# A planner's price for a change of the matmul tiling, extended to the second half of a four-layer kernel

## The chip, the cores and the metric

The kernel runs on one core of a Trainium2 chip. The metric is the device time of one execution in microseconds (us); where several executions are given, it is their median. Engines are named as in the profile: PE is TensorE (PEld its weight loads), DVE is VectorE, ACT is ScalarE, POOL is GpSimd, and SP issues most of the DMAs.

## The reference

A sequence of 2048 tokens of width 128 goes through four pre-norm layers. Each of them adds an attention-like block and then a feed-forward block to the stream `x`:

```python
x = L0_attn_x                                    # (1, 2048, 128), fp32
x = x + L0_attn(layernorm(x))                    # 16 heads of 8, softmax over all 2048 keys
x = x + L0_ffn(layernorm(x))                     # 128 -> 512 -> 128, gelu
x = x + L1_attn(layernorm(x))                    # 16 heads of 64, softmax over all 2048 keys
x = x + L1_ffn(layernorm(x))                     # gated, integer weights, 384 hidden
x = x + L2_attn(layernorm(x))                    # each token attends to itself and its two neighbours
x = x + L2_ffn(layernorm(x))                     # top-1 of 8 experts, 128 x 128
x = x + L3_attn(layernorm(x))                    # memory with a gradient step, a recurrence over
                                                 # chunks of 64 tokens: 32 chunks, in order
x = x + L3_ffn(layernorm(x))                     # top-2 of 8 experts and a shared one, 176 hidden
```

Everything after L1's attention is cheap for a token, but L3's memory makes the chunks wait for one another: chunk c starts from the state that chunk c-1 leaves.

## The kernel before

One Python function, `body`, writes the instructions of all engines. What it writes is fixed before anything runs, and each engine takes its instructions in the order in which they were written. That order comes from a planner inside `body`. The planner keeps an estimated clock for each engine (`clk["T"]` for TensorE, `A` for ScalarE, `D` for VectorE, `P` for GpSimd, `S` for DMA). All engine calls go through a wrapper (line 147, which is why every instruction in the profile has that line) that calls `note()` (line 96). `note()` prices the instruction, lets it start when its engine and its inputs are ready by the estimate, and moves that engine's clock. A matmul costs its columns at 2.4 GHz, four times that for fp32 inputs. The second matmul of a pair that runs in another part of the array is marked `par` and costs almost nothing.

Layer 0, with layer 1's keys and values, is the first half. The second half begins at line 951, where the accumulators' pools are made anew and the clocks are set to zero. Its skeleton is `l1_attn()` (line 1066): five blocks of queries (512, 388, 512, 384 and 256 columns; the 388 are 384 tokens and a few that neighbours need early) times eight pairs of heads give 40 units, numbered 0 to 39, and each unit has 16 groups, one for each 128 keys. The TensorE work of a group is:

- four pairs of score matmuls, with 64 rows to each (`qh,ka`, `ql,ka`, `qh,ka`, and `mbt,onr` for the maximum),
- one or two matmuls (`km,qh`) that look for the maximum of a unit ahead, whose result VectorE reduces into the tile `mx`,
- a pair for the values (`P,ka`, 128 rows by 64 columns, fp32, in two passes each).

ScalarE makes the exponentials `P`. GpSimd sums them into `acg`, and VectorE sums the last of them into `acd`.

Layers 1 (feed-forward), 2 and 3 are background work. They are generators: `stage_a` and `stage_a2` (layer 1's feed-forward, layer 2's projections), `stage_b` (the three-neighbour attention), `stage_b2` (layer 2's experts), `stage_c` (what the recurrence needs of 128 tokens), `chunk` (line 1626, one step of the recurrence, whose state is the tile `xst`), `stage_d` (its output), `stage_g` (the last router) and `s_lane` (line 1880). A lane job there is one of 13 slices of 128 hidden units of the last feed-forward, for 256 tokens: 8 blocks of 256 tokens times 13 make 104 jobs, whose input is the tile `xe`.

Each `yield` of a generator ends a piece. In every group `l1_attn` calls `fill()` (line 246) twice; it writes background pieces until TensorE's estimated clock has moved on by 0.3 us or until nothing may go. `may()` (line 202) lets a piece go by the clocks:

```python
if self.seen == len(emitted) or self.ready > clk["T"] + T["slack"]:
    return False
if max(clk["A"], clk["D"]) > clk["T"] + self.queue:
    return False
```

A piece is thus held back while its inputs would come later than TensorE's clock, or while ScalarE or VectorE is estimated to be further behind than `queue` (2.5 us, or 1.0 for the router, the lanes and the like). What is not written inside `l1_attn` is written after it by `drain()` (line 2018), with all accumulators and more lanes at hand. This last stretch is called the tail.

The flag `in0` decides whether `note()` charges TensorE 0.12 us where a matmul's shape on the array (rows and columns, each rounded up to 32, 64 or 128) differs from the one before. It is true in the first half; line 952 sets it to false for the second.

Of the kernel before, what the change touches and what calls it, by code (L numbers as in the profile page):

```python
# [70 lines left out]
def body(ctx: ExitStack, tc: tile.TileContext, x, pa, pb, pc, pi, pd, pr, pr0, pe, pw, out):  # L71
# [6 lines left out]
    def psum_pools(**n):  # L78
        psx.close()
        for k, bufs in n.items():  # L80
            PS[k] = psx.enter_context(tc.tile_pool(name=f"ps_{k}{bufs}", bufs=bufs, space=PSUM, reuse_waits="tile"))
# [5 lines left out]
    in0 = [True]  # L87
# [861 lines left out]
    rcd = dram.tile([48, 2, 512], F32, name="rcd")  # L949
    e0ctx.close()  # L950
    psum_pools(**T["ps"])
    in0[0] = False
    leave[0] = T["leave"]
    COST.update(L1COST)
    clk.update(dict.fromkeys("TADPS", 0.0))
# [1162 lines left out]
```

## Time and profile before

| | |
|---|---|
| median of 3 runs | 3005.0 us (2992.95 to 3006.38) |
| the profiled execution | 3001.08 us |
| its span, first instruction to last | 2999.2 us |
| PE busy | 2769.9 us (92%) |
| DVE busy | 2194.9 us (73%) |
| ACT busy | 1582.9 us (53%) |
| POOL busy | 1522.3 us (51%) |
| mean granted TensorE clock | 0.936 |

A line of a group of instructions gives the engine, the operation, out<-in by the program's tile names, and the shape. `64*128` before a matmul's shape is the part of the array that it uses, rows by columns. The accumulator of every matmul is called `mi`. A line of busy time by stage gives, for a stretch of the span, its length, then for each engine its busy us and (in brackets) its number of instructions, then the granted TensorE clock, the busy share of the DMA engines, and GB/s.

### The profile page before, as it was taken

The numbers are of one execution on the slowest core, as the hardware profiler recorded it, in microseconds if no ns is written. First come the engines' busy times: TensorE is split into PE (matmuls) and PEld (weight loads), VectorE is DVE, ScalarE is ACT, GpSimd is POOL, SyncE is SP. The second block draws the span as 40 slices with busy tenths as digits, with TensorE's granted clock in tenths as the row PEclk, the third lists the DMA queues.
The fourth block names the chain that finished last, engine by engine and source line by source line (L and its number), as shares of the span: only waits on it lengthen the run. The fifth ranks groups of instructions, "written<-read, shape, count | busy, mean of one in ns | idle before, by whom it ended". The sixth has DMA issues, their size and how long they took to land.

```text
span 2999.2 us, 49776 instructions
## 1 busy us (share of the span) xinstructions
PE 2769.9 (92%) x16719; PEld 1307.0 (44%) x16719; DVE 2194.9 (73%) x4699; ACT 1582.9 (53%) x3933; POOL 1522.3 (51%) x1762
## 2 busy tenths in 40 slices
PE   7999999999979899999999999899989898888998
PEld 2222222322234344454444444455544555565666
DVE  7899898898534666566666778887677769787765
ACT  1788887888854444444444444444434334333444
POOL 2400110201127688866776876677767556443444
PEclk9999999999979999999999999999999999776779
DMA  6311231321144333433442332233334343312244
GB/s 142 72 28 22 72 84 17 101 54 46 53 141 135 92 112 110 121 110 111 138 119 87 94 95 87 89 105 108 109 97 114 108 117 94 88 52 61 76 104 115
DMA packets 247749, 275.80 MB, mean 92 GB/s; under 512 B 95747, under 2 KB 183330, under 8 KB 247366
## 3 DMA queue, kind: packets, MB, share of 16 engines
q1 hardware_dynamic: 246630, 272.43, 33.2%
q8 instruction: 132, 2.16, 0.3%
q14 instruction: 123, 1.01, 0.1%
q10 hardware_dynamic: 864, 0.20, 0.0%
HBM read 229.97 MB, written 42.28 MB: 91 GB/s over the span
## 4 chain that ended last, share of the span: by engine, by line
PE 70%; DVE 18%; ACT 6%; issue 3%; DMA 3%; POOL 1%; SPq 0%; ACTq 0%; DVEq 0%; POOLq 0%
PE mi L147 70%; DVE mx L147 5%; ACT P L147 3%; DVE sB L147 1%; DVE o L147 1%; DVE gq L147 1%; DMA ka<-kvd 1%; DVE gt L147 1%; DVE xs L147 1%; ACT kf L147 1%; ACT kh L147 1%; DVE xn L147 1%; DVE sG L147 1%; DVE acd L147 1%; DVE sA L147 0%
## 5 line engine op out<-in xcount | busy, mean ns | idle before, releaser
L147 DVE TENSOR_REDUCE mx<-mi 128x1 f32<-128x512 f32 (+1 forms) x2080 | 1322.1, 683 | 582.8 <-PE mi L147 571.5
L147 ACT ACTIVATE P<-mi 128x512 f32<-128x512 f32 (+3 forms) x2304 | 1137.0, 551 | 1004.1 <-PE mi L147 973.2
L147 POOL TENSOR_TENSOR acg<-acg,P 128x512 f32<-128x512 f32 (+3 forms) x960 | 1011.4, 1083 | 181.8 <-ACT P L147 180.0
L147 PE MATMUL mi<-P,ka 128*64 128x512 f32 (+3 forms) x2560 | 597.6, 546 | 2.3 <-DVE mx L147 2.3
L147 PE MATMUL mi<-qh,ka 64*128 64x512 f32 (+3 forms) x2560 | 521.0, 406 | 9.7 <-DMA ka<-kvd 6.8
L147 PEld LDWEIGHTS mi<-qh,ka 64*128 64x128 f32 x2560 | 247.0, 189 | 382.5 <-issue 347.0
L147 PE MATMUL mi<-kop,qop 48*128 48x512 bf16 x1024 | 348.6, 405 | 24.5 <-DVE mx L147 12.1
L147 PE MATMUL mi<-qop,kop 50*128 50x512 bf16 x1024 | 317.8, 391 | 27.1 <-ACT P L147 24.7
L147 PE MATMUL mi<-P,vop 128*32 128x512 f32 x2048 | 304.3, 623 | 13.9 <-ACT P L147 13.9
L147 POOL TENSOR_SCALAR vep<-mv 128x2 f32<-128x2 f32 (+1 forms) x24 | 5.5, 229 | 495.6 <-DVE mv L147 495.6
L147 PE MATMUL mi<-km,qh 64*128 64x512 f32 x1024 | 225.6, 410 | 30.4 <-DVE mx L147 23.8
L147 PE MATMUL mi<-mbt,onr 64*128 64x512 f32 (+3 forms) x1280 | 228.7, 351 | 1.5 <-DMA mbt<-mb 1.5
L147 PE MATMUL mi<-ql,ka 64*128 64x512 f32 (+3 forms) x1280 | 229.2, 353 | 0.0
L147 PEld LDWEIGHTS mi<-P,ka 128*64 128x64 f32 x2560 | 129.2, 137 | 225.3 <-issue 195.1
L147 PEld LDWEIGHTS <-kop 50*128 50x128 bf16 x1024 | 63.6, 95 | 304.9 <-issue 281.6
L147 POOL TENSOR_TENSOR acg<-P 128x512 f32<-128x512 f32 (+3 forms) x80 | 91.1, 1158 | 202.5 <-DVE acd L147 162.0
L147 PEld LDWEIGHTS mi<-km,qh 64*128 64x128 f32 x1024 | 107.1, 189 | 60.5 <-DVE mx L147 38.5
L147 PEld LDWEIGHTS mi<-mbt,onr 64*128 64x128 f32 x1280 | 124.6, 190 | 13.9 <-DMA mbt<-mb 2.2
L147 PEld LDWEIGHTS mi<-ql,ka 64*128 64x128 f32 x1280 | 125.7, 192 | 0.0
L147 PEld LDWEIGHTS <-qop 48*128 48x128 bf16 x1024 | 72.9, 96 | 97.2 <-issue 82.7
L147 PEld LDWEIGHTS mi<-P,vop 128*32 128x32 f32 x2048 | 55.5, 109 | 119.8 <-issue 90.7
L147 POOL TENSOR_TENSOR kl<-kf,kh 128x512 f32<-128x512 f32 x32 | 40.9, 1278 | 110.9 <-ACT kh L147 82.4
(509 smaller groups left out, 3464.4 us busy)
## 6 DMA issues: line engine op xcount, KB each, us to landing
ka<-kvd SPq DMA_DIRECT2D x320, 384.0 KB
km<-khd SPq DMA_DIRECT2D x159, 256.0 KB
khd<-kh SPq DMA_DIRECT2D x32, 256.0 KB
kvd<-kh SPq DMA_DIRECT2D x32, 256.0 KB
kvd<-kl SPq DMA_DIRECT2D x32, 256.0 KB
kvd<-vt SPq DMA_DIRECT2D x16, 512.0 KB
ka<-in_pw_dram SPq DMA_DIRECT2D x37, 192.0 KB
w3s<-in_pw_dram SPq DMA_DIRECT2D x35, 192.0 KB
```

Of the source, the lines that this page charges most:

```text
L147: r = f(*a, **k)
```

## The change

One value is changed where the second half begins:

```diff
     e0ctx.close()
     psum_pools(**T["ps"])
-    in0[0] = False
+    in0[0] = True
     leave[0] = T["leave"]
     COST.update(L1COST)
     clk.update(dict.fromkeys("TADPS", 0.0))
```

The code in `note()` that the flag switches:

```python
if eng == "T" and in0[0]:
    m = tuple(min(c for c in (32, 64, 128) if c >= x) for x in (ins[0].shape[0], math.prod(ins[0].shape[1:])))
    d += 0.12 if m != mode[0] and not par else 0.0
    mode[0] = m
```

The estimate now counts 0.12 us at a change of the tiling in the second half too. No instruction's operands or arithmetic are touched directly; what the planner writes, and in which order, follows from the clocks.

## The prediction

> **What bounds the kernel now.** I read the page's busy rows and slices first, then busy time by stage, then the matmuls of one attention group in order of time, then the tail by what runs in it.
>
> ```profile
> PE 2769.9 (92%) x16719; PEld 1307.0 (44%) x16719; DVE 2194.9 (73%) x4699; ACT 1582.9 (53%) x3933; POOL 1522.3 (51%) x1762
> ...
> PE   7999999999979899999999999899989898888998
> ...
> PEclk9999999999979999999999999999999999776779
> ```
>
> TensorE is the busiest engine nearly throughout, and in the last 16% of the span its granted clock falls. The second half begins at 908.6 us (first matmul of unit 0) and its last score matmul ends at 2594.1. In the busy time by stage, the rows are units 16 to 23, 24 to 27, 28 to 31, 32 to 39, and then the tail, in which only background work is left:
>
> ```profile
> core 0: us, PE busy (x) PEld busy (x) DVE busy (x) ACT busy (x) POOL busy (x), PEclk, DMA share, GB/s
> 1542.30:1939.00 396.70, 377.32 (x2072) 169.89 (x2070) 307.53 (x556) 174.51 (x392) 289.64 (x250) 0.98 0.30 91
> 1939.00:2105.90 166.90, 162.83 (x1112) 87.31 (x1110) 126.54 (x278) 74.80 (x227) 115.10 (x132) 0.98 0.37 107
> 2105.90:2280.80 174.90, 163.19 (x1039) 84.41 (x1038) 119.63 (x242) 73.39 (x195) 120.68 (x141) 0.95 0.37 103
> 2280.80:2594.10 313.30, 283.26 (x2119) 162.63 (x2115) 243.17 (x605) 124.65 (x470) 191.23 (x292) 0.91 0.41 109
> 2594.10:2999.20 405.10, 345.36 (x1729) 257.05 (x1727) 290.15 (x1073) 160.88 (x662) 167.60 (x280) 0.76 0.31 79
> ```
>
> Attention is bound by TensorE: its idle time is 4 us of 167 in units 24 to 27 and 30 of 313 in units 32 to 39. The tail is mixed: PE 85% at clock 0.76, VectorE 72%, and through it runs the chunk recurrence, one step after another.
>
> One wide group (n = 512) of unit 3, matmuls alone:
>
> ```profile
> 1060.08 0.50 PE L147 MATMUL mi<-qh,ka 64*128 64x512 f32 x2
> 1060.42 0.39 PE L147 MATMUL mi<-ql,ka 64*128 64x512 f32 x2
> 1060.65 0.40 PE L147 MATMUL mi<-qh,ka 64*128 64x512 f32 x2
> 1060.87 0.40 PE L147 MATMUL mi<-mbt,onr 64*128 64x512 f32 x2
> 1061.10 0.40 PE L147 MATMUL mi<-km,qh 64*128 64x512 f32 x2
> 1061.43 1.08 PE L147 MATMUL mi<-P,ka 128*64 128x512 f32 x4
> 1062.44 0.51 PE L147 MATMUL mi<-qh,ka 64*128 64x512 f32 x2
> ```
>
> From start to start a pair takes 0.23 us, but 0.34 where the tiling has just changed (1060.08 to 1060.42) and 0.33 where it is about to (1061.10 to 1061.43). A change costs about 0.11 us, and the group 2.36.
>
> **What the change does to the estimate.** `note()` now adds 0.12 us at each change of shape that is not marked `par`. A wide group was priced 4 x 0.248 + 0.248 + 0.953 = 2.19 us; with two changes it is 2.43, against 2.36 measured. So far it mends the estimate. In units 32 to 39 (n = 256) the old price is 4 x 0.225 + 0.124 + 0.527 = 1.55 and the new one 1.79, where two groups take 2306.72 to 2309.46, thus 1.37 each: there the estimate was already high and gets higher. No instruction is added or taken out of the arithmetic. TensorE's estimated clock runs faster, VectorE's and ScalarE's look less behind, `may()` refuses less, and more background steps are listed inside attention.
>
> **What moves,** by the lists of the two built programs. The first half is unchanged. After the last attention group 798 background matmuls are listed, where there were 909. The recurrence has 13 chunks to begin there (before 18 of 32), `stage_d` 7 (before 10), and all 104 lane jobs stay in the tail in both. So the rows moved are small ones. I price each by its own mean start-to-start time, in two passes, in the tail and in attention:
> - five chunks (four for their last matmuls): 10.3 us of the tail, 8.8 us in attention;
> - three `stage_d`: 8.1 and 6.6;
> - three `stage_c`, and the router and normalization matmuls: 9.8 and 8.6;
> - lane jobs, which only change lanes: 0.
>
> Sum: TensorE loses 28.2 us in the tail and gets 24.0 in attention, switches into the rows included. VectorE has 861 instructions in the tail instead of 1,035, 16% of their summed time (379.3 to 318.8 us); ScalarE loses 17.2 us and GpSimd 16.3. Two places get most of it: units 20 to 23 (VectorE's summed durations 171.6 to 188.8 us) and 28 to 31 (121.0 to 166.3). The few DMA issues that move on SP (tail weights and router rows, past the key loads of two or three groups) I price at nothing: attention covers them, and TensorE waits for key loads some 21 us in all now; if that cover failed, it is a few us more.
>
> **The tail, from both sides.** If TensorE alone sets it, it shrinks in proportion: 28.2 x 405.1 / 345.4 = 33 us. If the recurrence sets it, five chunks go at their spacing. That spacing is in the answer for the state tile, and the lane jobs' pace in that for their input:
>
> ```profile
> L147 ACT COPY xst<-mi x18: 166/178/180, 2632.9 to 2924.9; 64x32 f32<-64x32 f32 x18
> ```
> ```profile
> 2594.10:2920.00 325.90, 101.65 (x294) 65.02 (x295) 2.21 (x6) 0.72 0.27 71
> 2920.00:2999.20 79.20, 40.42 (x152) 27.31 (x150) 0.37 (x1) 0.91 0.48 114
> ```
>
> (2924.9 - 2632.9) / 17 = 17.2 us a chunk, so 5 x 17.2 = 86 us. Neither is alone: after the recurrence ends, the lane matmuls run at 152 / 79.2 = 1.92 per us, before it at 294 / 325.9 = 0.90. With 13 chunks the first stretch is 13 / 18 x 331 = 239 us and does 0.90 x 239 = 215 of the 446 rows; the other 231 take 231 / 1.92 = 120 us. Together 359, a gain of about 46. I take 44, as TensorE's bound is the nearer, at 85% busy.
>
> The tail's clock belongs to this sum:
>
> ```profile
> 2760.00:2800.00 40.00, 39.84 (x173) 30.02 (x173) 24.91 (x94) 15.76 (x71) 16.20 (x28) 0.58 0.30 78
> ```
>
> TensorE was busy all through these 40 us, at clock 0.58. The prices above hold that low clock already: moved rows cost 28.2 us there and 24.0 in attention. The Trainium skill ("TensorE: Matmul & The Clock Gate", Part 1: The HAM clock gate) says that sustained activity releases the throttle, after about 3.4 us. By that rule alone a busy stretch runs at full clock, the moved rows would cost 24.0 us in both places, and the tail's lower bound would be an estimated 28 us; the row speaks against it, and the measured prices stand.
>
> **Attention.** Lower bound of what it gains in length: 24.0 us, as TensorE has no room. On top come stalls. In units 16 to 39 TensorE idles 65.2 us against 796.9 us of VectorE work, 0.082 per us; the moved VectorE work is 16% of the tail's 290.2, 46 us, thus 4 us. The other end is all 46 us on the path, where a group waits for its `mx` tiles behind background. I take 4: idling reached 10 to 14% only in units where VectorE is over 90% busy (32 and 37), and units 28 to 31 come to about 80% (busy time is 0.9 of summed durations: 166.3 x 0.9 / 187). Attention: +28.
>
> **Sum:** -44 + 28 = -16 us. The profiled execution took 3001.08 us (span 2999.2 and 1.9 around it); the runs' median is 3005.0, 0.13% above. 3001.1 - 16 = 2985 us.
>
> **Rivals.**
> - *The recurrence sets the tail.* For: the end follows its last step by 74 us, and its 17.2 us spacing hardly changes with the load. Against: 104 lane jobs remain. -86 + 28 = -58: 2943 us.
> - *TensorE's work is only moved.* For: 92% busy. Against: lane pace doubles when the recurrence is out of the way. -33 + 28 = -5: 2996 us.
> - *Slower: the estimate runs too far ahead in units 32 to 39.* There it is now 31% above the measured group, before 13%. Steps are then listed before their inputs exist, and TensorE, which takes its list in order, waits with the score matmuls queued behind; ScalarE's exponentials wait for those. For: these units already idle 30.0 us of 313.3, the worst of attention. Against: the amount listed there rises little (28 matmuls). If idling grows with the error, 30 x 31 / 13 = 72, +42 us; with the tail at its lower bound, -33 + 24 + 42 = +33: 3034 us. It decides once TensorE idles over some 50 us there.
> - That the change does nothing is excluded: the lists differ from the second half's second unit on.
>
> **How the numbers follow.** A measurement of this kernel can tell about 0.5% (15 us) from no change. My forecast, 40%, own range -45 to +10 us (faster 0.27, same 0.11, slower 0.02). Recurrence 12%, faster. Work only moved 16% (same 0.13, faster 0.01, slower 0.02). Stalls 32%, slower. Together faster 0.40, same 0.24, slower 0.36. The range goes from beyond the recurrence's 2943 to beyond the stalls' 3034, as the unknown 46 us of VectorE work could add to that: 2940 to 3045.
>
> **What would show it.** Right: the last score matmul ends near 2594 + 28 = 2622, the tail is near 361 us with 14 state copies, and units 28 to 31 grow from 175 us while TensorE stays over 90% busy. The recurrence rival shows as a tail of about 320 us. The moving rival shows as a tail of 372. The slower one shows as units 32 to 39 well over 330 us, with TensorE under 85% busy and waits for DVE tiles at its head. Wrong altogether: a change in the first 908 us, or of more than a few us in units 0 to 15.

## The result, and the profile after

The changed kernel takes 3099.64 us in the median of 4 runs (3080.73 to 3106.37), the kernel before 3004.75 us in the runs beside them: a ratio of 1.0314 [1.0262, 1.0367], 3% slower. The prediction was 2985 us, 0.5% faster than before, so it had the wrong sign. The profiled execution took 3098.06 us (span 3096.3, against 2999.2), and its mean granted clock was 0.927 (0.936).

The row of busy times on the changed kernel's page, to be set beside that of before:

```profile
PE 2803.7 (91%) x16719; PEld 1321.1 (43%) x16719; DVE 2225.3 (72%) x4699; ACT 1581.6 (51%) x3936; POOL 1523.5 (49%) x1762
```

The number of matmuls is the same, PE is busy 34 us longer, and the span grew by 97. The busy time by stage says where. First units 2 to 6 of the kernel before, which the prediction took to be untouched:

```profile
999.90:1207.30 207.40, 207.40 (x1173) 89.20 (x1171) 127.93 (x201) 100.79 (x188) 167.83 (x131) 1.00 0.36 110
```

and of the changed kernel units 2 to 6, 16 to 23, 24 to 27, 28 to 31, 32 to 39, and the tail:

```profile
995.00:1228.30 233.30, 216.41 (x1173) 92.28 (x1171) 148.75 (x201) 99.35 (x188) 165.01 (x131) 0.96 0.33 98
1567.60:1993.70 426.10, 395.18 (x2165) 179.76 (x2163) 323.30 (x625) 178.92 (x437) 295.05 (x263) 0.96 0.28 85
1993.70:2169.00 175.30, 164.66 (x1101) 88.32 (x1099) 131.55 (x267) 77.34 (x219) 125.19 (x143) 0.97 0.34 102
2169.00:2375.00 206.00, 182.11 (x1104) 95.36 (x1102) 166.66 (x358) 78.09 (x237) 126.58 (x149) 0.93 0.31 87
2375.00:2725.40 350.40, 312.52 (x2174) 180.62 (x2172) 226.99 (x621) 127.20 (x487) 190.20 (x296) 0.82 0.34 98
2725.40:3096.30 370.90, 308.18 (x1525) 228.42 (x1525) 248.09 (x884) 147.60 (x569) 152.18 (x244) 0.78 0.34 86
```

The tail shrank as it was meant to, 405.1 to 370.9 us. Attention grew from 1685.5 to 1820.3 us: 26 us in units 2 to 6, 29 in 16 to 23, 8 in 24 to 27, 31 in 28 to 31, 37 in 32 to 39, and 3 in the rest. The instruction counts of units 2 to 6 are the same in both rows. There was no more work, and yet TensorE, which had not paused once in 207.4 us at clock 1.00, now waits, and runs at 0.96.

I split TensorE's time in attention by the start-to-start times of its matmuls into attention's own rows, background rows, and idle:

| us | before | after | change | predicted |
|---|---|---|---|---|
| idle | 78.9 | 137.5 | +58.6 | +4 |
| attention's own rows (unchanged) | 1311.4 | 1350.0 | +38.6 | 0 |
| background rows | 295.5 | 333.1 | +37.6 | +24.0 |
| sum | 1685.8 | 1820.6 | +134.8 | +28 |

Of the 69 us in units 16 to 31, 30 are idle, 28 background rows (147 more matmuls in the trace) and 10 attention's own rows. Of the 26 in units 2 to 6, which hold no more background, 17 are idle and 7 attention's own rows.

**A stall in units 2 to 6.** The same multiply of the same unit, `o` by `rb` (the end of a unit's softmax, written by a generator in the unit after it). In the timeline of before, VectorE's, GpSimd's and TensorE's steps around it:

```profile
1066.03 0.76 DVE L147 TENSOR_TENSOR o<-o,rb 128x512 f32<-128x512 f32 x1 [0.83 <-DMA rb<-rcd]
...
1066.21 1.72 POOL L147 TENSOR_TENSOR acg<-acg,P 128x512 f32<-128x512 f32 x1
...
1068.03 0.19 DVE L147 TENSOR_REDUCE m<-mx 128x8 f32<-128x32 f32 x1
...
1068.55 0.38 PE L147 MATMUL mi<-ident,m 128*4 128x128 f32 x2
```

and in the timeline of the changed kernel:

```profile
1061.19 9.92 POOL L147 TENSOR_TENSOR acg<-acg,P 128x512 f32<-128x512 f32 x8
...
1065.91 5.75 DVE L147 TENSOR_TENSOR o<-o,rb 128x512 f32<-128x512 f32 x1 [0.25 <-DMA rb<-rcd]
...
1071.58 0.17 DVE L147 TENSOR_REDUCE m<-mx 128x8 f32<-128x32 f32 x1
...
1071.81 0.38 PE L147 MATMUL mi<-ident,m 128*4 128x128 f32 x2 [4.08 <-DVE m L147]
...
1073.08 0.63 PE L147 MATMUL mi<-mbt,onr 64*128 64x512 f32 x2
1073.51 0.63 PE L147 MATMUL mi<-km,qh 64*128 64x512 f32 x2
...
1074.07 1.97 PE L147 MATMUL mi<-P,ka 128*64 128x512 f32 x4
...
1074.54 2.50 POOL L147 TENSOR_TENSOR acg<-acg,P 128x512 f32<-128x512 f32 x2 [3.43 <-ACT P L147]
```

The multiply takes 5.75 us instead of 0.76. GpSimd's first row holds the last eight of a run of 18 sums back to back, which ends at 1061.19 + 9.92 = 1071.11; the multiply ends 0.55 us later. VectorE's next step, `m`, is late by that, and TensorE waits 4.08 us for it, because the transposition of `m` stands at the head of its list.

The single sums show what the multiply waits for. In each of units 2 to 6 of the kernel before, it ends 0.55 us after the sum that was under way when it began, and GpSimd's next sum takes 1.71 or 1.72 us instead of about 1.27: the two engines take turns. In the same units of the changed kernel it ends 0.55 or 0.56 us after the last sum of the run, and no sum in between takes longer: VectorE gets its turn only when GpSimd has run out of work. GpSimd's next sum then waits 3.4 to 5.5 us (3.43 here) for exponentials, as ScalarE waits for TensorE's scores (6.13 us here).

Then comes the second cost: TensorE's rows run at half pace (0.43 us from start to start instead of 0.23, the value pair 1.97 instead of 1.08) until about 1075.97. In units 2 to 6 this multiply took 0.73 to 1.67 us before and 4.56 to 6.08 after. With the price the list has it one group later; in four of these five units it begins 1.8 to 3.9 us later into the unit, in the fifth 0.4 us earlier.

The Trainium skill ("SBUF — State Buffer", 🔬 SBUF: two separate sides) has VectorE and GpSimd share a pair of ports under an exclusive lock, held for a whole instruction, and a VectorE operation with two inputs in SBUF competes for it with a GpSimd operation that reads SBUF. The kernel before agrees: the multiply waits for the end of one sum. The changed kernel agrees in kind but not in size: the lock of one instruction would be an estimated 1.24 us here (9.92 / 8), and after the sum under way VectorE waited through four more.

**A stall in units 32 to 39,** in the timeline of the changed kernel:

```profile
2586.77 5.21 DVE L147 TENSOR_SCALAR dz<-dzr,rr 64x32 f32<-64x32 f32 x1
...
2589.19 2.75 POOL L147 TENSOR_TENSOR acg<-acg,P 128x256 f32<-128x256 f32 x4
...
2592.04 0.42 PE L147 MATMUL mi<-dz,kcs 64*64 64x32 f32 x2 [3.99 <-DVE dz L147]
```

Here a background matmul of the recurrence is listed before its input exists. `dz` (0.24 us in the median of its 32) ends at 2591.98, with GpSimd's run at 2591.94; TensorE waits 3.99 us with the score matmuls of the next group behind it. The busy time of the 4.8 us after it:

```profile
2592.60:2597.40 4.80, 4.80 (x23) 2.65 (x22) 1.70 (x6) 0.66 (x2) 0.00 (x0) 0.50 0.08 20
```

TensorE is busy without a break, at clock 0.50. A wait of 4 us is thus followed by several more at half pace.

### The profile page after: what moved, and what is told of

Its sections match the earlier page's. It is cut to its first block, busy times and chain, and to the rows that moved or that the text cites. A ratio compares the mean times of both kernels' runs of the same rounds, so it can differ in the third digit from the quotient of the medians.

```text
span 3096.3 us, 49758 instructions
## 1 busy us (share of the span) xinstructions
PE 2803.7 (91%) x16719; PEld 1321.1 (43%) x16719; DVE 2225.3 (72%) x4699; ACT 1581.6 (51%) x3936; POOL 1523.5 (49%) x1762
## 5 line engine op out<-in xcount | busy, mean ns | idle before, releaser
L147 PE MATMUL mi<-P,ka 128*64 128x512 f32 (+3 forms) x2560 | 613.4, 559 | 2.2 <-DVE mx L147 1.9
L147 PE MATMUL mi<-qh,ka 64*128 64x512 f32 (+3 forms) x2560 | 533.4, 416 | 1.6 <-DMA ka<-kvd 1.6
L147 PEld LDWEIGHTS mi<-qh,ka 64*128 64x128 f32 x2560 | 254.1, 195 | 374.5 <-issue 350.6
L147 DVE TENSOR_TENSOR o<-o,rb 128x512 f32<-128x512 f32 (+3 forms) x40 | 70.9, 1773 | 46.9 <-DMA rb<-rcd 46.8
```

Of the source, the lines that this page charges most:

```text
L147: r = f(*a, **k)
```

## The experiments

"Trace rows" are background matmuls counted in the trace; "rows left" are those listed after the last attention group (909 before, 798 after). Stage lengths are from one profiled execution each, ratios from timed runs beside the kernel before. Two executions with the same list of TensorE differ too: by 6 us in units 32 to 39 (before and `e4`), by 8 in units 16 to 23 and by 9 in the tail (the changed kernel and `e9`), so a few us in one stage say little. The shared base of `e1` to `e4` is the kernel before (`in0` false at line 952), and the flag is then set where the edit says.

**The price in units 0 to 7 alone**

```diff
             u, k = divmod(g, 16)
+            in0[0] = 0 <= u < 8
...
         do_merge()
+        in0[0] = False
```

> The price of 0.12 us counts in units 0 to 7 alone; everything after unit 7 is listed as in the kernel before. Own stages: if the loss adds up stage by stage, as the two traces have it, units 0 to 7 take 24 us more (363.3 against 338.9) and nothing else changes: 3029 us. One cause at the end: if the whole loss comes from the background steps that are pulled forward later on, these units cost nothing by themselves: 3005 us, within 8.

3016.35 us, ratio 1.0067 [1.0036, 1.0098], between the two forecasts. Units 2 to 6, in its busy time by stage:

```profile
996.60:1218.60 222.00, 210.94 (x1174) 90.06 (x1171) 140.39 (x201) 99.32 (x188) 165.99 (x131) 0.98 0.35 103
```

These units lose 14.6 us (207.4 to 222.0) without one more background row, over half of the 25.9 us that the full change loses there. Three waits over 2 us stand in them; before had none, and the full change has five.

**The price in units 16 to 31, and in units 32 to 39, alone**

```diff
             u, k = divmod(g, 16)
+            in0[0] = 16 <= u < 32      # the other kernel: 32 <= u < 40
...
         do_merge()
+        in0[0] = False
```

> The price counts in units 16 to 31 alone. 812 background matmuls are left for the tail instead of 909, so nearly all of the shift is in this kernel. Own stages: units 16 to 31 grow by 69 us as in the changed kernel (807.5 against 738.6), the tail falls by 30: 3044 us. If instead the loss is from the too dear groups of units 32 to 39, this one shows only the shift that was forecast, about -30 + 25: 3000 us.

> The price counts in units 32 to 39 alone (256 columns, where the estimate is 31% too dear with it); 877 matmuls are left for the tail. Own stages: +37 us in these units, -10 in the tail: 3032 us. If these groups' wrong price is the main cause of all: +70 or more, 3075 us. If the loss lies in the shift from the units before: 3005 us.

The first: 3034.91 us, 1.0125 [1.0092, 1.0159]; units 16 to 23 take 425.0 us, 24 to 27 175.1, 28 to 31 208.3, within 2.5 us of the full change each, and the tail 371.6. The second: 3006.86 us, 1.0038 [1.0010, 1.0066]; units 32 to 39 take 353.5 us at clock 0.85, and the tail 374.6. The total of the second is that of its last forecast (3005), but by luck: these units lost 40 us, and the tail gained 31 instead of 10. So each stage's loss comes from the price in that stage, and each of the two alone already gains the tail's 31 to 34 us. The gains do not add up, the losses do. By single executions, the spans of `e1`, `e2` and `e3` grew by 14.8, 31.1 and 4.8 us, 51 together. With the tail's gain counted once instead of twice (31 us) that is 82, and with the 11 us that units 2 to 6 lose beyond `e1`, 93 of the 97.

**The price in the tail alone**

```diff
         do_merge()
+        in0[0] = True
```

> The price counts in the tail alone; all 640 attention groups are listed as in the kernel before. If the order within the tail plays a part, the 405 us of the tail change by 10 us or more either way; by the traces, in which the tail's length follows its TensorE work alone, it stays within 6 us: 3005 us.

2995.01 us, 0.9989 [0.9962, 1.0016]: no difference. What the price does to the order within the tail is not what matters.

**As much work moved, without the price.** `queue` is raised, so `may()` lets ScalarE and VectorE be further behind:

```diff
-lim=0.3, backlog=2.5,
+lim=0.3, backlog=3.0,
...
-    in0[0] = True
+    in0[0] = False
```

> No price in the second half; instead a background piece may go while VectorE or ScalarE is up to 3.0 us behind by the estimate, not 2.5. 813 background matmuls are left for the tail, close to the 798 of the changed kernel, so as much is moved into attention by another door. Amount: if any background that is added to attention costs what it cost in the changed kernel, units 16 to 39 grow by some 100 us and the tail falls by 33: 3070 us. Early listing: if the loss is that the priced clock lets steps go before their inputs exist, these steps (still judged by the slow clock) cost their own TensorE time, about 25 us, and the tail falls by 33: 2995 us.

2981.96 us, 0.9911 [0.9886, 0.9936], 0.9% faster. 813 rows are left (798 in the change). Its units 16 to 39 and its tail:

```profile
1537.30:2631.20 1093.90, 1016.57 (x6507) 524.95 (x6504) 844.11 (x1830) 458.22 (x1373) 726.34 (x844) 0.94 0.36 97
2631.20:2983.80 352.60, 297.24 (x1551) 221.99 (x1549) 258.22 (x923) 149.53 (x576) 154.64 (x249) 0.82 0.36 90
```

Units 16 to 39 grew by 42 us for nearly the work that costs 106 in the change (1051.8 to 1157.8), and the tail shrank by 52. Moving work into attention pays, then; it is the way in which the price moves it that does not. The comparison is cleanest in units 32 to 39: 105 trace rows more cost 17.5 us here (313.3 to 330.8), 55 rows more cost 37 us in the change, and 57 cost 40 in `e3`. In units 24 to 31, 55 rows more cost 19 us here and 52 cost 39 in the change.

**The price, with a margin on every input.** `sem`, the delay that the estimate adds to each result before others may use it, goes up, so a step is listed later:

```diff
-sem=0.2,
+sem=0.35,
```

> The price counts in the whole second half, and the estimate lets every result be ready 0.35 us after its instruction instead of 0.2. 914 matmuls are left for the tail, as many as before the change (909). Amount: 3003 us, with the tail back at 405. Early listing: the margin of 0.15 us per step is small beside the waits of several us seen in the changed kernel, so some of the idle time in units 16 to 39 stays (10 to 20 us above the 65 of before), and units 2 to 6 keep their loss: 3030 us.

3027.24 us, 1.0074 [1.0046, 1.0102]. Units 16 to 39 take 1057.5 us, 100 less than with the price alone; but 914 rows are left and the tail takes 416.5 us. That is near its second forecast, and idle time in units 16 to 39 is 12 us above that of before, as it said. But the margin undid the move as well as most of the stalls, so this run alone does not part the two. Units 2 to 6 still take 237.6 us: that loss has another cause.

**The multiply on GpSimd, in three kernels.** In units 0 to 7 `o` times `rb` is taken from VectorE. It then stands in line with the sums that it collided with:

```diff
-        ve.tensor_tensor(o[:, :n], o[:, :n], rb[:, :n], ALU.mult)
+        (Eng(nc.gpsimd, "D") if u < 8 else ve).tensor_tensor(o[:, :n], o[:, :n], rb[:, :n], ALU.mult)
```

on the kernel with the price in units 0 to 7, on the kernel before, and on the changed kernel:

> The price counts in units 0 to 7 alone, as in e1_units0to7, and the multiplication of o by rb in these units runs on GpSimd, at the same place in the plan and at VectorE's price; TensorE's list is the same row for row. Held by GpSimd: if VectorE's multiplication took 5 to 6 us because GpSimd's back-to-back sums held what both need, units 2 to 6 come back from 222 to 207 us and unit 1 loses its 9 us too: 2992 us. Place alone: if what costs is only that the step stands a group later, units 2 to 6 stay at 222: 3015 us.

> The kernel before, with the multiplication of o by rb in units 0 to 7 on GpSimd. Held by GpSimd: unit 1's 8.9 us of idle TensorE goes, all else stays: 2992 us. If GpSimd, at 79 to 87% busy in these units, becomes the bound with 1.3 us more in each: 3005 to 3012 us.

> The changed kernel (price in the whole second half), with the multiplication of o by rb in units 0 to 7 on GpSimd. If the loss of units 1 to 6 adds to the rest: units 0 to 6 fall from 323 us to 290, the rest stays: 3065 us. If the loss there was a loan (the later units would wait instead): 3090 us or more.

Measured 2990.07 us (0.9954 [0.9927, 0.9980]), 2989.86 (0.9956 [0.9933, 0.9980]) and 3061.73 (1.0226 [1.0185, 1.0268]). Each came within 4 us of the first of its two forecasts. Units 2 to 6 of the third:

```profile
987.00:1196.10 209.10, 207.99 (x1173) 89.31 (x1171) 123.11 (x196) 99.46 (x188) 174.62 (x139) 1.00 0.36 109
```

TensorE's list in attention is that of the changed kernel row for row, and the 26 us are gone with the price still on: idle falls from 16.9 to 1.1 us, and attention's own rows, which nothing touched, from 196.3 to 189.7. On GpSimd the multiply takes 1.28 us. That shows it for units 2 to 6: the collision caused the waits, and four of the five waits in the changed kernel cost a stretch at a low clock besides (0.50 to 0.66 in the 5 us after them; 1.00 after the 2.91 us of unit 2). In the kernel before, the 10.9 us multiply of unit 1 goes the same way (units 0 to 1 from 91.3 to 80.6 us).

**The price, with the narrow matmuls' estimate fitted.** In the second half the least price of a matmul that isn't fp32 goes from 0.19 to 0.11 us. A group of 256 columns is then priced 1.46 us instead of 1.79, where 1.37 was measured:

```diff
-                d = max(d, 0.19) + 0.015
+                d = max(d, low[0]) + 0.015
...
     in0[0] = True
+    low[0] = 0.11
```

> The price counts in the whole second half, and the least price of a score matmul is lowered from 0.19 to 0.11 us there, so that a group of 256 columns is estimated at 1.46 us (measured 1.37) instead of 1.79, and one of 384 at 1.9. 862 matmuls are left for the tail. Too dear narrow groups: if this is what lets steps go too early there, units 32 to 39 come back from 350 us to about 315 and units 24 to 31 lose half of their 39 us; the tail at about 390: 3060 us. If the price alone does it, with whatever the narrow groups are held to cost, units 24 to 39 stay 70 us longer than before: 3095 us.

3070.70 us, 1.0257 [1.0210, 1.0304]. Units 32 to 39:

```profile
2364.60:2667.10 302.50, 273.93 (x2122) 158.60 (x2119) 211.11 (x543) 123.38 (x475) 184.87 (x286) 0.92 0.42 113
```

They fall from 350.4 to 302.5 us, under the 313.3 of before with five background rows more, and at clock 0.92 instead of 0.82. They hold 50 rows fewer than in the change, but that is not the reason: `e5` has 50 more than the change there and takes 330.8 us. So there the slower rival's cause holds: with the estimate fitted, the loss is gone. The whole misses its forecast by 11 us (the profiled execution, 3064.51 us, by 5): units 16 to 27 stay as slow as in the change or slower (421.8 and 182.5 us), and the tail is 25 us longer than there.

**Half the price,** 0.06 us, in both halves:

```diff
-                d += 0.12 if m != mode[0] and not par else 0.0
+                d += 0.06 if m != mode[0] and not par else 0.0
```

> A change of the tiling is priced at 0.06 us in the whole kernel's both halves instead of 0.12 in the first and none in the second. 859 matmuls are left for the tail, about half of the shift. If the loss grows with how far the estimated clock is put ahead: half of 95 us, 3050 us. If it turns on whether single steps fall a group early or late: units 2 to 6 either keep their 15 to 26 us or lose nothing, and the total is anywhere between 3005 and 3060.

2998.88 us, 1.0003 [0.9978, 1.0028]: no difference, and less than both forecasts. 859 rows are left, and the tail takes 375.4 us, nearly all of the gain. Units 32 to 39 take 315.7 us with 68 trace rows more than before, and units 2 to 6 215.7, with one wait over 2 us. A group of 256 columns is priced 1.67 us here, still 22% above the measured 1.37, and next to nothing is lost there. The loss is not in proportion to the price, nor to the error of the estimate.

**The two that help, together:** `queue` at 3.0 without the price, and the multiply on GpSimd in units 0 to 7.

```diff
-lim=0.3, backlog=2.5,
+lim=0.3, backlog=3.0,
...
-        ve.tensor_tensor(o[:, :n], o[:, :n], rb[:, :n], ALU.mult)
+        (Eng(nc.gpsimd, "D") if u < 8 else ve).tensor_tensor(o[:, :n], o[:, :n], rb[:, :n], ALU.mult)
```

> No price in the second half, a queue of 3.0 us as in e5_queue3_no_price, and the multiplication of o by rb in units 0 to 7 on GpSimd as in e8_before_o_on_gpsimd. The two act in different units: -26 and -13 us, thus 2966 us. If they meet (the tail or GpSimd sets the end): 2980 us.

2960.75 us, 0.9886 [0.9852, 0.9919], the fastest of all and faster than both kernels. Units 2 to 6 take 207.4 us, with TensorE busy in all of them, and the tail 352.8 us at clock 0.82.

**Side by side.** Gaps over 2 us between TensorE's matmuls in units 2 to 6 and 16 to 39, the length of attention, and that of the tail:

| kernel | gaps | their sum, us | attention, us | tail, us |
|---|---|---|---|---|
| before | 6 | 26 | 1685.5 | 405.1 |
| price in units 0 to 7 (`e1`) | 11 | 41 | 1696.6 | 410.6 |
| queue 3.0, multiply on GpSimd (`e11`) | 9 | 29 | 1702.3 | 352.8 |
| price and margin (`e6`) | 13 | 49 | 1706.9 | 416.5 |
| half price (`e12`) | 11 | 40 | 1708.7 | 375.4 |
| price in units 32 to 39 (`e3`) | 10 | 36 | 1722.2 | 374.6 |
| queue 3.0 (`e5`) | 11 | 39 | 1723.1 | 352.6 |
| price in units 16 to 31 (`e2`) | 18 | 62 | 1751.6 | 371.6 |
| price, narrow fitted (`e10`) | 19 | 64 | 1761.3 | 395.7 |
| price, multiply on GpSimd (`e9`) | 19 | 65 | 1791.0 | 379.7 |
| after | 25 | 82 | 1820.3 | 370.9 |

The four kernels with 18 gaps or more have the four longest attentions. A short tail does not need them: `e5` and `e11` have the shortest tails of all, with 11 and 9 gaps.

## Why the prediction was wrong, point by point

The step that failed is the length of attention: forecast +28 us, measured +134.8. It had the stalls too small, left out the low clock after them, and held a stage untouched that was not; that work moves and that the tail shrinks was right.

- **"Wrong altogether: a change ... of more than a few us in units 0 to 15."** That came about: 26 us in units 2 to 6. The prediction had priced what moved between attention and the tail, and took a stage in which no background row moved as unchanged. There a single VectorE step of each unit moved by one group, and GpSimd held it up. `e1`, `e7` and `e9` show it.
- **The term of 4 us for stalls measured +58.6 us.** I sized it by the share of VectorE's time in which TensorE idles, and let it grow only where VectorE is over 90% busy. In units 28 to 31 VectorE is busy for 166.7 us of 206.0, 81% as forecast, and they lost 31 us all the same. A wait does not need a busy engine; one late result at the head of TensorE's list is enough. In units 16 to 39, which this term was for, idle time grew by 38.1 us (65.2 to 103.3), near the upper end of 46 that I had named and not near the 4 that I took; the other 20 us are in units 0 to 15.
- **A term was missing: the clock after a stall, +38.6 us.** I used the granted clock for the tail only, and took attention's own rows at their price of before. After a wait of about 4 us they run at half pace for some microseconds. The mean granted clock of attention fell from 0.97 to 0.94. In units 32 to 39 this is most of the loss: of 37 us, 22.4 are attention's own rows (191.8 to 214.2), 7.0 background rows and 7.9 idle. The Trainium skill's rule on the throttle ("TensorE: Matmul & The Clock Gate", Part 1: The HAM clock gate) gives a throttled array half its clock, and about 3.4 us of activity to release it. The rows after the two stalls shown agree in the half (0.50); the first recovers in about 3.5 us, the second takes more than the 4.8 us of its row.
- **Background rows, 24.0 us, measured +37.6.** I priced each by its mean start-to-start time in attention of before, at that clock; the lower clock may raise that too. How much of the 13.6 us is the clock alone I did not separate.
- **The tail, -44, measured -34.2.** That is near TensorE's bound of the prediction (-33), but partly by luck: TensorE's busy time in the tail fell by 37.2 us (345.36 to 308.18), not the 28.2 that I priced, and its idle time, which the bound lets shrink in proportion, grew by 3 us (59.7 to 62.7). The state copies after the last score matmul became 14, as predicted, but their spacing grew with the lane jobs around them. In the answer for the state tile in the tail, and in the busy time of the matmuls on `xe` until the last state copy and after it:

```profile
L147 ACT COPY xst<-mi x14: 178/179/180, 2728.6 to 2982.4; 64x32 f32<-64x32 f32 x14
```
```profile
2725.40:2982.40 257.00, 72.44 (x208) 46.17 (x208) 1.47 (x4) 0.69 0.23 60
2982.40:3096.30 113.90, 57.36 (x232) 39.76 (x232) 0.72 (x2) 0.96 0.59 144
```

  (2982.4 - 2728.6) / 13 = 19.5 us a chunk, where I took 17.2 to hold. The first stretch is 257 us instead of 239; the second, 114 instead of 120, was right. So the recurrence rival, with its tail of 320 us, fell too; the tail came out as the moving rival's, 372.
- **The slower rival had the right place and sign, and nearly the size, for another reason.** I said +42 us of idle time in units 32 to 39; they grew by 37, but with TensorE 89% busy, not under 85%, since it is paid in clock. `e10` shows the estimate as the cause there, though by `e12` an estimate 22% too high costs next to nothing. I had given 32% to it and set it in one stage; units 16 to 31 lost 69 us more, and `e2` shows that the price there does it. The prediction took the wide groups' better estimate (2.43 against 2.36 us) as harmless.
- **Right:** the first half unchanged (unit 0 starts at 905.1 us, before 908.6), which rows move, and that moving them can pay: `e5` moves as much and gains.

What stays open: why GpSimd's sums hold a VectorE step through several instructions in some groups and through hardly one in others (at 1066.03 us before, GpSimd was working back to back as well); how the loss of units 16 to 23 divides between amount and moment, since its growth per trace row is the same 0.3 us with the price (95 rows, 29 us) and with the longer queue (19 rows, 5.6 us), but 0.6 us at half price (23 rows, 13 us); why half the price loses nothing in units 32 to 39; why the tail lost 31 us in `e3` for 57 trace rows of 1719; and why it is shorter in `e5` than in the change, for fewer rows moved.

## What to carry to other kernels

In a list that an engine takes in order, a price that is right for one instruction can make the whole estimate worse; compare the estimated with the measured time of a whole group in every stage before adding to it. Count the waits over 2 us at the head of the busiest engine, and price each at the wait and the slow stretch behind it; a busy share hides both. Where VectorE and GpSimd both work without a break, a VectorE step with no urgent reader can still hold up everything queued behind it, and may be cheaper on GpSimd itself.

## What the runs showed of the hardware

- A 128x512 multiply on VectorE took 0.76 us in one place and 5.75 us in another. In the first it ended 0.55 us after one GpSimd sum, and GpSimd's next sum took 1.72 us instead of 1.27; in the second it ended 0.55 us after the last sum of a run, which had gone on over it. A 64x32 step took 5.21 us instead of 0.24 and ended with GpSimd's run too. Moved to GpSimd, the multiply took 1.28 us. In the whole of units 16 to 39, however, such VectorE steps (over 1.5 us above the usual time of their form) add up to 51 us before, 69 in the change, and 70 in the faster `e5` too: there they are a part of the cause and not the measure of it.
- After a wait of about 4 us, TensorE ran at a granted clock of 0.50 for several microseconds although it was busy throughout. In the changed kernel's units 2 to 6 and 16 to 39, 23 of the 25 waits of over 2 us were followed by a mean clock of at most 0.66 over the next 5 us, and two by 1.00 (waits of 2.91 and 2.04 us). In all five stages with more waits the clock fell, from 1.00 to 0.96 in units 2 to 6 and from 0.91 to 0.82 in units 32 to 39.
